# Attention with a depthwise convolution in the queries: low halves ahead of hops, second sums ahead of convolution, fewer taps beside the batches

## The chip, the cores and the metric

The kernel runs on one core of one Trainium2 chip. The metric is device time in microseconds (us) of one execution. A core has TensorE (PE in the rows; PEld is its weight load), VectorE (DVE), ScalarE (ACT), GpSimd (POOL) and SyncE (SP), each with an instruction queue of its own that is worked off in order, and 16 DMA engines that all the issuing queues share. A row marked SPq is SyncE's queue issuing a transfer.

## The reference

All of it is float32: four images of 384 channels and 48 x 48 = 2304 tokens, eight heads of 48 channels.

```python
local = conv(x, conv_w, 7x7, SAME, one filter per channel)       # then scaled and shifted by bn
x_norm = layernorm(x over channels)                              # at each token
q, k, v = split(x_norm @ qkv_w.T + qkv_b)                        # 8 heads of 48
q = q + layernorm(local over channels)
attn = softmax(q @ k.T * 48 ** -0.5)
out = x + (attn @ v) @ proj_w.T + proj_b
```

## The kernel before

**Groups and batches.** Each image's queries are cut into five groups of 8, 10, 10, 10 and 10 rows of 48 tokens (384 or 480 columns). There are 20 groups, t = 0 to 19; image b has groups 5b to 5b + 4. A group works through four pairs of heads with 18 blocks of 128 keys each, in eight batches s = 0 to 7 of nine blocks; pair p has batches 2p and 2p + 1. In a batch TensorE first makes the scores (L1152): keys and queries are split into a high half, which the matmul's short format holds, and the low half that remains, so a block takes six matmuls and nine blocks take 54. ScalarE turns the scores into exponentials (L1168, L1164); in groups from 4 on, DVE copies one half block out of its bank (L1172), and ScalarE works on that copy later. Then TensorE weighs the values with the exponentials (L1189, 36 rows in the profile). Eight banks, taken two at a time, hold the scores.

**Quarters.** The rest of the work is hung into the batches by hand. `steps_of(t)` lists, for batch s and quarter q, what is issued at `(s, q)`: quarter 0 in the middle of the scores, 1 behind the scores, 2 in the middle of the weighing, 3 behind it. TensorE's order is not affected by the quarters' DVE work, but a wait is.

**Key stages.** Between the images ("kv" in the code, t = 5, 10, 15) six groups gk of 384 tokens are projected to values, keys and queries (`from_x`, L730), and the image before gets its output projection and residual (L1126). Each gk has five places h = 0 to 4 for convolution.

**Convolution on DVE.** The 7 x 7 filter is 49 multiply-adds ("taps", L374) per channel chunk, 144 instructions a group after ScalarE's first ones. A planner spreads all 2659 that remain after start-up: `spare` and `spare_at_keys` say how many us of DVE time a quarter or place has beside its other work, in units that are scaled by the group's columns, `due` says by which place a group's taps must be done, and `share` is the number of taps that result.

**The queries' norms.** A query group's convolution is normalized over channels. Groups 1 to 4 take their means by matmul. The groups t + 1 of later images (t = 5 to 8, 10 to 13, 15 to 18) take sums by a *hop*: `sum` (L597, L598), a 32 x 32 transpose and a reduction (L678, L679), then two small transfers on SyncE's queue, `parts<-part` (L682) into DRAM and `four<-parts` (L683) back to all partitions; the second waits on SyncE until the first has landed. DVE then adds the four (L692). There is a first hop for the mean (`q_sum`, read by `few_centre`) and a second for the variance (`sum_squares` and `out`, read by `few_variance`); `few_root` is three small ScalarE instructions (L711 to L713), `few_newton` finishes the root on DVE (L717 to L719), `local_end` (L982) scales, `query_end` (L994) adds the projected query. The norm of the next image's x goes the same way in the key stages and in some groups.

**Query parts.** `high_queries` casts one pair's queries to the short format on ScalarE (L1008); `low_queries` subtracts on DVE (L1013) and issues six transfers (L1018, L1020), on SyncE's queue except for some of the first groups, that put both halves where the matmuls read them (tile qs). Pair p's parts are made during batch 2p - 2, pair 0's at the end of the group before.

**Sums.** The softmax denominators of group t - 1 go through DRAM: den out (L1061), rd in (`sums_in`, L1072), reciprocal and check (L1082, L1086), rden out and rb in (`divide`).

Of the kernel before, what the change touches and what calls it, by code (L numbers as in the profile page):

```python
# [49 lines left out]
def unshifted_pass(  # L50
# [21 lines left out]
    G = RG * W  # L72
# [8 lines left out]
    NA = len(ROWS)  # L81
# [380 lines left out]
    def spare(t, s, q):  # L462
# [4 lines left out]
        time -= {(0, 3): 0.5, (2, 3): 0.5, (4, 3): 0.5}.get((s, q), 0.0)  # L467
        if b + 1 < B and g >= begins(b + 1):
            time -= {
                (1, 3): 2.3, (3, 1): 2.2, (3, 3): 2.3, (5, 0): 0.4, (5, 2): 2.6,  # L470
            }.get((s, q), 0.0)
        if g:
            time -= {(1, 2): 0.6, (5, 1): 1.4}.get((s, q), 0.0)
        if t + 1 < NA:
# [4 lines left out]
            time -= {(6, 3): 3.0, (7, 0): 1.0, (7, 2): 0.5}.get((s, q), 0.0)  # L479
        elif g < NA - 1:  # L480
            time -= {
                (2, 2): 2.3, (4, 0): 2.2, (4, 3): 2.3, (6, 0): 0.4, (6, 2): 2.8, (6, 3): 1.7,
                (7, 0): 0.5,
            }.get((s, q), 0.0)
        return max(0.3, time) * columns_of(t) / G
# [9 lines left out]
    def spare_at_keys(b, g, h):  # L495
        time = 4.6 - {0: 0.6, 2: 0.7, 3: 1.4, 4: 1.2}.get(h, 0.0)
# [30 lines left out]
    share = {}  # L527
# [702 lines left out]
    def steps_of(t):  # L1230
# [13 lines left out]
        for p in range(1, NP):  # L1244
            at(2 * p - 2, 1, lambda p=p: high_queries(t, p))
            at(2 * p - 2, 3, lambda p=p: low_queries(t, p))
        if g:

            def begin():
                ratios[t] = divide(t - 1)  # L1250
# [5 lines left out]

            at(1, 2, begin)
# [34 lines left out]
        if following:  # L1292
# [11 lines left out]
            at(2, 2, q_sum)  # L1304
# [3 lines left out]
            at(6, 0, lambda: norm.few_variance())  # L1308
            at(6, 1, lambda: norm.few_root())
            at(6, 2, q_end)  # L1310
            at(6, 3, lambda: high_queries(t + 1, 0))
            at(7, 0, lambda: low_queries(t + 1, 0))
        if early:
# [26 lines left out]
            at(7, 2, lambda: low_queries(t + 1, 0, other))  # L1340
# [143 lines left out]
    for t in range(NT):  # L1484
        b, g = divmod(t, NA)
        if g == 0 and b:
# [3 lines left out]
            norms_x = {}  # L1490
            for gk in range(NG):
# [25 lines left out]
                if gk == 5:  # L1517
                    norm.few_variance()
                    norm.few_root()
# [3 lines left out]
                convolve("kv", t, gk, 1)  # L1523
# [22 lines left out]
                convolve("kv", t, gk, 4)  # L1546
# [585 lines left out]
```

## Time and profile before

| What | Value |
|---|---|
| Median of 3 runs | 2731.15 us (2725.64 to 2733.86) |
| Profiled execution | 2727.67 us, span 2725.8 us |
| TensorE busy | 2701.5 us, 99% |
| DVE busy | 2345.3 us, 86% |
| ScalarE busy | 1651.8 us, 61% |
| Taps (L374) | 2832, mean 657 ns |

Busy times say how long an engine had an instruction under way. The span is the time from the first to the last instruction. A releaser behind an arrow is what ended a wait; `DMA qs<-qs` is the landing of a transfer that wrote qs. A wait that TensorE does not share costs nothing by itself. TensorE's granted clock is 0.999 over the span.

### The profile page before, as it was taken

The page shows a single profiled execution, that of the slowest core. Times are in us where ns is not written, and L with a number is a line of the kernel's source. Part 1 is how long each engine was busy: PE and PEld are TensorE (multiplying, and loading weights), DVE is VectorE, ACT ScalarE, POOL GpSimd, SP SyncE. Part 2 cuts the span into 40 slices and gives each one's busy share as a digit, 9 for nine tenths or more (in the row PEclk, how much of TensorE's full clock was granted, in tenths as well). Part 3 has the DMA queues.
Part 4 walks back from the last instruction along what each step waited for, and adds up shares of the span by engine and source line. Part 5 has one row for each costly group of instructions (what it writes and reads, how often), then busy time and mean ns, then how long its engine had stood idle before and what let it go on. Part 6 is the DMA issues. An engine that isn't in the chain of part 4 may idle for free.

```text
span 2725.8 us, 45553 instructions
## 1 busy us (share of the span) xinstructions
PE 2701.5 (99%) x16468; PEld 1546.6 (57%) x16468; DVE 2345.3 (86%) x4090; ACT 1651.8 (61%) x2478; POOL 592.1 (22%) x1061
## 2 busy tenths in 40 slices
PE   9999999999999999999999999999999999999999
PEld 6565555555556555555555665555555665555555
DVE  8999999899989999989999999988898899996212
ACT  4366666677325766777632677776752376776662
POOL 3531111112462111010255210101115511101110
PEclk9999999999999999999999999999999999999999
DMA  8454544546456545354555553545635645445442
GB/s 176 91 148 138 136 116 123 135 128 163 109 154 163 140 118 149 109 147 123 149 140 141 167 139 116 140 131 128 157 107 162 164 123 142 135 131 145 133 135 89
DMA packets 160124, 370.42 MB, mean 136 GB/s; under 512 B 58273, under 2 KB 107234, under 8 KB 159890
## 3 DMA queue, kind: packets, MB, share of 16 engines
q0 software_dynamic: 70688, 277.77, 36.2%
q1 hardware_dynamic: 83456, 79.29, 12.8%
q10 hardware_dynamic: 5746, 10.36, 1.2%
q8 instruction: 132, 2.16, 0.4%
q14 instruction: 102, 0.84, 0.1%
HBM read 258.14 MB, written 64.14 MB: 118 GB/s over the span
## 4 chain that ended last, share of the span: by engine, by line
PE 81%; DVE 11%; DMA 5%; SPq 1%; issue 1%; ACT 1%; POOL 0%; DVEq 0%; ACTq 0%; POOLq 0%
PE banks L1189 35%; PE banks L1152 30%; PE banks L730 15%; DVE acc L374 7%; DMA qs<-qs 1%; DMA parts<-part 1%; DMA four<-parts 1%; DMA rd<-den 1%; SPq L1020 0%; DVE pt L841 0%; DVE sq L598 0%; DVE pt L1172 0%; DMA qt<-xn 0%; DVE sq L597 0%; DVE xn L994 0%
## 5 line engine op out<-in xcount | busy, mean ns | idle before, releaser
L374 DVE SCALAR_TENSOR_TENSOR acc<-slab,vec,acc 128x470 f32<-128x470 f32 (+10 forms) x2832 | 1656.5, 657 | 0.4 <-ACT acc L337 0.4
L1189 PE MATMUL banks<-pt,v 128*64 128x480 f32 (+1 forms) x5760 | 1150.1, 553 | 0.0
L1168 ACT ACTIVATE pt<-banks 128x960 f32<-128x960 f32 (+1 forms) x1152 | 1008.2, 946 | 131.1 <-PE banks L1152 78.2
L1152 PE MATMUL banks<-qs,ks 64*128 64x480 f32 (+1 forms) x8640 | 965.2, 374 | 13.1 <-DMA qs<-qs 9.7
L1152 PEld LDWEIGHTS banks<-qs,ks 64*128 64x128 f32 x8640 | 790.3, 184 | 242.1 <-issue 116.5
L1189 PEld LDWEIGHTS banks<-pt,v 128*64 128x64 f32 x5760 | 399.9, 137 | 672.6 <-issue 629.9
L802 POOL DMA_DIRECT2D ks<-wide x220 | 159.8, 726 | 1409.1 <-PE banks L1152 1386.3
L1164 ACT ACTIVATE pt<-banks 128x480 f32<-128x480 f32 (+1 forms) x448 | 256.5, 572 | 141.3 <-PE banks L1189 141.3
L730 PE MATMUL banks<-xn,w_qk 128*128 128x384 f32 x864 | 284.2, 486 | 0.0
L730 PEld LDWEIGHTS banks<-xn,w_qk 128*128 128x128 f32 x864 | 164.0, 190 | 114.7 <-issue 0.7
L1172 DVE COPY pt<-banks 128x480 f32<-128x480 f32 (+1 forms) x128 | 81.6, 638 | 147.3 <-PE banks L1152 145.4
L1037 ACT COPY o<-banks 113x480 f32<-113x480 f32 (+1 forms) x80 | 43.6, 545 | 196.2 <-PE banks L1189 196.1
L730 PE MATMUL banks<-w_v,xn 128*128 128x384 f32 x432 | 145.1, 488 | 3.5 <-DVE xn L725 3.0
L824 ACT COPY v<-banks 128x384 f32<-128x384 f32 x72 | 34.3, 478 | 165.8 <-PE banks L730 165.8
L1047 ACT COPY ao<-banks 113x480 f32<-113x480 f32 (+1 forms) x60 | 32.7, 545 | 141.5 <-PE banks L1189 141.5
L730 PEld LDWEIGHTS banks<-w_v,xn 128*128 128x128 f32 x432 | 81.3, 190 | 62.8 <-DVE xn L725 4.7
L730 PE MATMUL banks<-af,w_o 128*128 128x384 f32 (+1 forms) x270 | 85.2, 470 | 0.0
L1056 DVE TENSOR_TENSOR ao<-ao,o 113x480 f32<-113x480 f32 (+1 forms) x60 | 38.0, 633 | 54.3 <-ACT o L1037 54.3
L787 POOL DMA_DIRECT2D wide<-pt x120 | 59.9, 502 | 108.6 <-ACT pt L838 101.4
L1164 ACT ACTIVATE pt<-pt 128x480 f32<-128x480 f32 (+1 forms) x128 | 80.8, 632 | 0.6 <-DVE pt L1172 0.6
L838 ACT ACTIVATE pt<-banks,qkb 128x384 fp32r<-128x384 f32 x60 | 34.6, 581 | 60.3 <-PE banks L730 55.9
L730 PEld LDWEIGHTS banks<-af,w_o 128*128 128x128 f32 x270 | 51.3, 190 | 31.9
(160 smaller groups left out, 1450.1 us busy)
## 6 DMA issues: line engine op xcount, KB each, us to landing
ks<-wide POOLq DMA_DIRECT2D x220, 768.0 KB, 5.4
qs<-qs SPq DMA_DIRECT2D x346, 60.0 KB
slab<-in_x_dram POOLq DMA_DIRECT2D x22, 432.0 KB, 7.9
wide<-ks POOLq DMA_DIRECT2D x12, 768.0 KB, 5.4
xr<-in_x_dram POOLq DMA_DIRECT2D x16, 576.0 KB, 5.1
rb<-rden SPq DMA_DIRECT2D x32, 270.0 KB
held<-ao POOLq DMA_DIRECT2D x12, 720.0 KB, 4.5
xn<-in_x_dram POOLq DMA_DIRECT2D x36, 216.0 KB, 5.3
```

What stands on the lines that cost most here:

```text
L374: nc.vector.scalar_tensor_tensor(dst, src, weight, dst, ALU.mult, ALU.add)
L730: nc.tensor.matmul(dst, lhsT=weights(c), rhs=src(c), start=c == 0, stop=c == CC - 1)
L787: nc.gpsimd.dma_start(out=last[16 * u : 16 * u + 16, 0], in_=k[r : r + 16, 0])
L802: queue.dma_start(out=place_keys(b, p, i), in_=wide[b, p][:, :, at])
L838: nc.scalar.activation(k[:, 0, :], r[:, :G], AF.Identity, bias=bias)
L1037: nc.scalar.copy(part[0 : 64 + HA], sums[0 : 64 + HA, :n])
L1056: nc.vector.tensor_add(dst, dst, part[0 : 64 + HA])
L1152: nc.tensor.matmul(r[:, j, :n], lhsT=ks[rows, w, at], rhs=qs[rows, m, :], start=n_th == 0, stop=n_th == 2,)
L1164: nc.scalar.activation(weights_of[:, at, :n], src, AF.Exp, scale=SCALE)
L1168: nc.scalar.activation(to, r[:, :, :n], AF.Exp, scale=SCALE)
L1172: nc.vector.tensor_copy(weights_of[:, second, :n], r[:, 1, :n])
L1189: nc.tensor.matmul(sums[halves[j], :n], lhsT=values[t // NA, kb // NB][:, first : first + 64], rhs=weights_of[:, at[j], :n], start=start, ...
```

## The change

1. Low halves of pairs 1 to 3 are issued at quarter 2 of batches 0, 2 and 4 instead of quarter 3, and the query norm's first hop (`q_sum`) at quarter 3 of batch 2 instead of quarter 2.
2. Pair 0 of groups 1 to 4: low halves in the middle of quarter 1's convolution in batch 7 instead of quarter 2. Of the groups with hops: variance at (5, 3) instead of (6, 0), root and end of the query both at (6, 1) instead of (6, 1) and (6, 2), high half at (6, 2) and low half at (6, 3) instead of (6, 3) and (7, 0).
3. `sums_in` is called at (0, 3), `divide` still at (1, 2).
4. Key stages: the second sums and their hop ahead of place 4's convolution, variance and root in the middle of place 1's convolution instead of ahead of it.
5. The planner's costs follow these moves; every quarter from group 5 on has 0.1 less, every place of a key stage 0.2 more.

```diff
         if q == 0:
             time -= 0.5 * (s % 2 == 0) + 0.5 * (t >= NA - 1)
-        time -= {(0, 3): 0.5, (2, 3): 0.5, (4, 3): 0.5}.get((s, q), 0.0)
+        time -= {(0, 2): 0.5, (2, 2): 0.5, (4, 2): 0.5}.get((s, q), 0.0)
...
         elif g < NA - 1:
             time -= {
-                (2, 2): 2.3, (4, 0): 2.2, (4, 3): 2.3, (6, 0): 0.4, (6, 2): 2.8, (6, 3): 1.7,
-                (7, 0): 0.5,
+                (2, 3): 2.5, (4, 0): 2.2, (4, 3): 2.5, (5, 3): 0.4, (6, 1): 2.6, (6, 2): 2.0,
+                (6, 3): 0.5,
             }.get((s, q), 0.0)
-        return max(0.3, time) * columns_of(t) / G
+        time = max(0.3, time) - (0.1 if t >= NA else 0.0)
+        return time * columns_of(t) / G
...
     def spare_at_keys(b, g, h):
-        time = 4.6 - {0: 0.6, 2: 0.7, 3: 1.4, 4: 1.2}.get(h, 0.0)
+        time = 4.8 - {0: 0.6, 2: 0.7, 3: 1.4, 4: 1.2}.get(h, 0.0)
...
-            last = "slot", t - 1, 2, 2
+            last = "slot", t - 1, 2, 3
...
             at(2 * p - 2, 1, lambda p=p: high_queries(t, p))
-            at(2 * p - 2, 3, lambda p=p: low_queries(t, p))
+            at(2 * p - 2, 2, lambda p=p: low_queries(t, p))
         if g:
 
+            def sums():
+                ratios[t] = sums_in(t - 1)
+
             def begin():
-                ratios[t] = divide(t - 1)
+                ratios[t] = divide(t - 1, ratios[t])
...
+            at(0, 3, sums)
             at(1, 2, begin)
...
-            at(2, 2, q_sum)
+            at(2, 3, q_sum)
             at(4, 0, lambda: norm.few_centre())
             at(4, 2, lambda: norm.squares())
             at(4, 3, lambda: norm.sum_squares(), lambda: norm.out())
-            at(6, 0, lambda: norm.few_variance())
-            at(6, 1, lambda: norm.few_root())
-            at(6, 2, q_end)
-            at(6, 3, lambda: high_queries(t + 1, 0))
-            at(7, 0, lambda: low_queries(t + 1, 0))
+            at(5, 3, lambda: norm.few_variance())
+            at(6, 1, lambda: norm.few_root(), q_end)
+            at(6, 2, lambda: high_queries(t + 1, 0))
+            at(6, 3, lambda: low_queries(t + 1, 0))
...
             at(7, 1, lambda: high_queries(t + 1, 0))
-            at(7, 2, lambda: low_queries(t + 1, 0, other))
+            halfway[t, 7, 1] = lambda: low_queries(t + 1, 0, other)
...
                 both(making)
-                if old:
-                    old.few_variance()
-                    old.few_root()
...
-                convolve("kv", t, gk, 1)
+
+                def variance():
+                    for n in (old, norm if gk == 5 else None):
+                        if n:
+                            n.few_variance()
+                            n.few_root()
+
+                convolve("kv", t, gk, 1, at=made + share["kv", t, gk, 1] // 2, then=variance)
...
-                convolve("kv", t, gk, 4)
                 if new is not None:
                     norms_x[gk].sum_squares()
                     norms_x[gk].out()
                 if gk == 4:
                     norm.sum_squares()
                     norm.out()
+                convolve("kv", t, gk, 4)
```

**SyncE's queue, group 13, batches 1 to 3.** The first fence is the kernel before, the second the changed one, whose line numbers are one higher here (L1019 is L1018 before). `qs_2` is the third pair's tile; the 4x32x15 hop is the query norm's, the 4x32x12 one is that of the next image's x.

```order
L1061 DMA den_15502<-ao_15500 1x480 x2
L682 DMA parts<-part 4x32x15
L683 DMA four<-parts 128x1x60
L1018 DMA qs_2_15716<-qs_2_15716 16x960
L1020 DMA qs_2_15716<-qs_2_15716 32x480 x2
L1018 DMA qs_2_15716<-qs_2_15716 16x960
L1020 DMA qs_2_15716<-qs_2_15716 32x480 x2
L682 DMA parts<-part 4x32x12
```

```order
L1062 DMA den_15504<-ao_15502 1x480 x2
L1019 DMA qs_2_15711<-qs_2_15711 16x960
L1021 DMA qs_2_15711<-qs_2_15711 32x480 x2
L1019 DMA qs_2_15711<-qs_2_15711 16x960
L1021 DMA qs_2_15711<-qs_2_15711 32x480 x2
L683 DMA parts<-part 4x32x15
L684 DMA four<-parts 128x1x60
L683 DMA parts<-part 4x32x12
```

The six qs transfers and the norm's first hop have changed places. In all of SyncE's queue this happens twelve times and nothing else moves; `rd<-den` stands where it stood.

**DVE, group 11, batch 6 into batch 7.** The kernel before, then the changed one. L1172 (L1173) is the copy that opens a batch, L717 to L719 the Newton step, `qs_0` the next group's first pair.

```order
L1172 COPY pt<-banks 128x480
L692 TENSOR_REDUCE few<-four 128x15
L706 TENSOR_SCALAR few<-few 128x15
L374 SCALAR_TENSOR_TENSOR acc_13182<-slab_3_12457,vec,acc_13182 128x10x47 x7
L717 TENSOR_TENSOR few_u<-few_u,few 128x15
L718 SCALAR_TENSOR_TENSOR few_y<-few_u,few_y 128x15
L719 STREAM_TRANSPOSE sq<-few_y 128x480
L982 SCALAR_TENSOR_TENSOR acc_11986<-acc_11986,sq 128x1440
L994 SCALAR_TENSOR_TENSOR xn<-acc_11986,vec,xn 128x480 x3
L374 SCALAR_TENSOR_TENSOR acc_13182<-slab_3_12457,vec,acc_13182 128x10x47 x3
L1172 COPY pt<-banks 128x480
L1013 TENSOR_TENSOR qs_0_14276<-xn,qs_0_14276 128x480
```

```order
L1173 COPY pt<-banks 128x480
L374 SCALAR_TENSOR_TENSOR acc_13168<-slab_3_12400,vec,acc_13168 128x10x47 x3
L718 TENSOR_TENSOR few_u<-few_u,few 128x15
L719 SCALAR_TENSOR_TENSOR few_y<-few_u,few_y 128x15
L720 STREAM_TRANSPOSE sq<-few_y 128x480
L983 SCALAR_TENSOR_TENSOR acc_12013<-acc_12013,sq 128x1440
L995 SCALAR_TENSOR_TENSOR xn<-acc_12013,vec,xn 128x480 x3
L374 SCALAR_TENSOR_TENSOR acc_13168<-slab_3_12400,vec,acc_13168 128x10x47 x2
L1014 TENSOR_TENSOR qs_0_14263<-xn,qs_0_14263 128x480
L374 SCALAR_TENSOR_TENSOR acc_13168<-slab_3_12400,vec,acc_13168 128x10x47 x5
L1173 COPY pt<-banks 128x480
```

The variance (L692, L706) has left the batch, the Newton step has three taps ahead of it instead of seven, and the low half has come in ahead of batch 7's copy.

**DVE, image 1's key stage, from gk = 2 into gk = 3.** Before, then changed. `sq<-sq` starts the second sums, L692 with L706 is the variance, `sq<-xn` the next norm's first sum.

```order
L597 TENSOR_TENSOR sq<-sq 128x384
L598 TENSOR_TENSOR sq<-sq 128x384
L678 STREAM_TRANSPOSE sq<-sq 128x384
L679 TENSOR_REDUCE part<-sq 128x12
L1126 SCALAR_TENSOR_TENSOR xr_2_6251<-banks,pb,xr_2_6251 128x384 x2
L374 SCALAR_TENSOR_TENSOR acc_5309<-slab_1_4789,vec,acc_5309 128x10x46 x3
L597 TENSOR_TENSOR sq<-xn 128x384
L598 TENSOR_TENSOR sq<-sq,xn 128x384
L678 STREAM_TRANSPOSE sq<-sq 128x384
L679 TENSOR_REDUCE part<-sq 128x12
L692 TENSOR_REDUCE few<-four 128x12
L706 TENSOR_SCALAR few<-few 128x12
```

```order
L679 STREAM_TRANSPOSE sq<-sq 128x384
L680 TENSOR_REDUCE part<-sq 128x12
L374 SCALAR_TENSOR_TENSOR acc_5240<-slab_1_4723,vec,acc_5240 128x10x45 x2
L1127 SCALAR_TENSOR_TENSOR xr_2_6264<-banks,pb,xr_2_6264 128x384 x2
L374 SCALAR_TENSOR_TENSOR acc_5240<-slab_1_4723,vec,acc_5240 128x10x45 x3
L598 TENSOR_TENSOR sq<-xn 128x384
L599 TENSOR_TENSOR sq<-sq,xn 128x384
L679 STREAM_TRANSPOSE sq<-sq 128x384
L680 TENSOR_REDUCE part<-sq 128x12
L374 SCALAR_TENSOR_TENSOR acc_5240<-slab_1_4723,vec,acc_5240 128x10x45 x3
L693 TENSOR_REDUCE few<-four 128x12
L707 TENSOR_SCALAR few<-few 128x12
```

Two taps of place 4 have moved behind the reduction that starts the hop, and three of place 1 ahead of the variance. The three key stages have 92, 103 and 100 taps before and 103, 117 and 113 in the change.

More of the change, by code (lines that the diff above doesn't have):

```diff
@@ L466, in spare @@
             time -= 0.5 * (s % 2 == 0) + 0.5 * (t >= NA - 1)
-        time -= {(0, 3): 0.5, (2, 3): 0.5, (4, 3): 0.5}.get((s, q), 0.0)
+        time -= {(0, 2): 0.5, (2, 2): 0.5, (4, 2): 0.5}.get((s, q), 0.0)
         if b + 1 < B and g >= begins(b + 1):
             time -= {
-                (1, 3): 2.3, (3, 1): 2.2, (3, 3): 2.3, (5, 0): 0.4, (5, 2): 2.6,
+                (1, 3): 2.5, (3, 1): 2.2, (3, 3): 2.5, (5, 0): 0.4, (5, 2): 2.6,
             }.get((s, q), 0.0)
         if g:
-            time -= {(1, 2): 0.6, (5, 1): 1.4}.get((s, q), 0.0)
+            time -= {(1, 2): 0.8, (5, 1): 1.4}.get((s, q), 0.0)
         if t + 1 < NA:
@@ L1490, in unshifted_pass @@
             norms_x = {}
+            norm = None
             for gk in range(NG):
```

5 lines of the change are left out of this document (1 added, 4 removed).

## The prediction

> **What bounds the kernel now.** First the page's busy times by engine, then two rows of the waits (us in all, times, longest us).
>
> ```profile
> PE 2701.5 (99%) x16468; PEld 1546.6 (57%) x16468; DVE 2345.3 (86%) x4090; ACT 1651.8 (61%) x2478; POOL 592.1 (22%) x1061
> ...
> PE banks L1152 <- DMA qs<-qs: 9.7, 13, 1.6
> ...
> PE banks L1152 <- DVE pt L1172: 2.3, 2, 1.7
> ```
>
> TensorE sets the end: it was idle for 24.3 of 2725.8 us. What it waited for belongs to this change: late query parts (qs) and late copies out of its banks (pt). Since the ends of matmuls are modelled, I size each loss by the distance of starts. The chain of waits in order of time (start, us, what) shows an undisturbed batch and three disturbed places:
>
> ```profile
> 1016.02 7.40 PE banks L1189 x36
> ...
> 1053.20 8.80 DMA rd<-den
> ...
> 1072.17 7.40 PE banks L1189 x36
> ...
> 1166.25 7.40 PE banks L1189 x36
> ...
> 1194.63 8.23 DMA qs<-qs
> 1208.82 7.40 PE banks L1189 x36
> ...
> 1752.79 6.05 PE banks L1152 x54
> 1758.84 7.40 PE banks L1189 x36
> ...
> 1826.07 7.40 PE banks L1189 x36
> 1842.97 8.16 DMA parts<-part
> 1855.01 9.07 DMA qs<-qs
> 1871.38 7.40 PE banks L1189 x36
> ```
>
> A batch takes 6.05 (scores) + 7.40 (weighing) = 13.45. In group 13 the weighing of batches 1 and 4 starts 45.31 apart, three batches (40.35) and 5.0 lost. In group 8 it is 42.57: 2.2 lost. From group 6's batch 6 to group 7's batch 2 it is 56.15 for four batches: 2.4 lost, behind the sums' transfer (rd). Smaller losses stand in TensorE's own order of time:
>
> ```profile
> 360.49 0.48 PE L1152 MATMUL banks<-qs,ks 64*128 64x480 f32 x1
> 361.60 0.70 PE L1152 MATMUL banks<-qs,ks 64*128 64x480 f32 x4 [0.62 <-DMA qs<-qs]
> 362.64 1.56 PE L1152 MATMUL banks<-qs,ks 64*128 64x480 f32 x12 [0.34 <-DMA qs<-qs]
> ...
> 811.68 6.07 PE L730 MATMUL banks<-w_v,xn 128*128 128x384 f32 x18 [2.41 <-DVE xn L725]
> ...
> 880.60 0.79 PE L1152 MATMUL banks<-qs,ks 64*128 64x384 f32 x5
> 882.08 4.66 PE L1152 MATMUL banks<-qs,ks 64*128 64x384 f32 x49 [0.69 <-DMA qs<-qs]
> ...
> 926.55 0.91 PE L1152 MATMUL banks<-qs,ks 64*128 64x480 f32 x5
> 928.09 5.64 PE L1152 MATMUL banks<-qs,ks 64*128 64x480 f32 x49 [0.63 <-DMA qs<-qs]
> ...
> 954.50 4.38 PE L1152 MATMUL banks<-qs,ks 64*128 64x480 f32 x37
> 959.43 2.22 PE L1152 MATMUL banks<-qs,ks 64*128 64x480 f32 x17 [0.55 <-DVE pt L1172]
> 961.59 7.47 PE L1189 MATMUL banks<-pt,v 128*64 128x480 f32 x36
> ```
>
> A score matmul of 480 columns takes 6.05/54 = 0.112. As group 2 opens, five of them from 360.49 should be out by 361.05, but the sixth starts at 362.64: 1.6 lost.
>
> **Part 1, the third pair's low halves ahead of the norm's first hop (groups 5 to 8, 10 to 13, 15 to 18).** Group 13 again, DVE's and the queue's rows:
>
> ```profile
> 1843.38 0.65 DVE L1013 TENSOR_TENSOR qs<-xn,qs 128x480 fp32r<-128x480 f32 x1
> ...
> 1851.81 0.58 SPq L1018 DMA_DIRECT2D qs<-qs  x1
> ...
> 1867.00 0.24 DVE L692 TENSOR_REDUCE few<-four 128x15 f32<-128x60 f32 x1
> ```
>
> The halves were ready at 1844.03, but SyncE stood at the hop's second transfer until its first had landed (8.16 from 1842.97), and issued them from 1851.81. In the changed order they are ahead of the hop: 7.8 earlier, and the subtraction itself comes a quarter earlier. That covers the 5.0, the 2.2, and in group 5 another 1.1 (five matmuls of 384 columns, at 0.112 x 384/480 = 0.09, end 0.45 after 880.60, but the next starts 1.48 after it). Gain 8.3. Bounds: 0, if the transfers' own 8 to 9 us set the end, and 8.3. I take 8.3, since the 7.8 of standing is more than any of the losses.
>
> What is late next is the hop. It starts behind six more issues (0.58 each, 3.5) and, as a quarter is some four taps and the low half, about 3 later. Its reader came 24.0 after the start (1842.97 to 1867.00) and keeps about 17. The longest hop that a DVE wait lets one measure took 9.0 (part 4). Price 0; a hop that took all of the 24 would hold DVE for 7, in groups 8 and 13.
>
> **Part 2, the first pair's low halves.** They move, for groups 1 to 4, from batch 7's third quarter into the middle of its second, and for the groups whose norm uses hops from batch 7 into batch 6's last quarter. In groups 0, 1 and 2 the orders have two, three and four convolution taps fewer ahead of them: at 0.63 a tap (part 4) 1.3, 1.9 and 2.5 earlier. The next groups' openings lost 2.0, 1.6 and 1.4, read as the 1.6 above. Gain 1.3 + 1.6 + 1.4 = 4.3. At group 6 five matmuls from 926.55 end at 927.11 and the sixth starts at 928.09, 1.0 lost; the halves now leave some 3 earlier. Gain 5.3 in all, bounds 2.5 (half the lead arrives) and 5.3.
>
> **Part 3, sums fetched a batch sooner.** In SyncE's order the rd transfer stands behind the same six qs transfers as before, so it issues when it did, at 1053.20. Price 0; bounds -1 and 1, as DVE's order around it shifts by a tap or two (0.63 each).
>
> **Part 4, the second sums ahead of convolution, and the variance in the middle of it (key stages).** Before, DVE came to the hop's result too soon; the last two rows group image 1's key stage by line (count, busy us, mean ns, idle before).
>
> ```profile
> 790.03 0.58 SPq L682 DMA_DIRECT2D parts<-part  x1
> ...
> 799.04 0.23 DVE L692 TENSOR_REDUCE few<-four 128x12 f32<-128x48 f32 x1 [3.92 <-DMA four<-parts]
> ...
> L374 DVE SCALAR_TENSOR_TENSOR acc<-slab,vec,acc 128x470 f32<-128x470 f32 (+3 forms) x109 | 68.6, 694 | 0.0
> L692 DVE TENSOR_REDUCE few<-four 128x12 f32<-128x48 f32 x10 | 2.3, 227 | 12.6 <-DMA four<-parts 12.6
> ```
>
> A tap is 68.6/109 = 0.63. Between hop and reader stood 9.0 - 3.9 = 5.1 of DVE work. Now the two taps that stood before the hop and three or four of the next share stand there too: 5.1 + 6 x 0.63 = 8.9, about the hop. So most of the 12.6 idle us become work, and the xn that TensorE had to wait 2.41 for at 811.68 comes some 3 earlier. Gain 2.4, bounds 0 and 2.4.
>
> [...]
>
> **Part 5, the planner.** The orders move 11, 14 and 13 taps out of the batches into the three later key stages: 6.9, 8.8 and 8.2 us of DVE. Those stages by windows (from:to, us, then busy of PE, PEld, DVE, ACT, POOL):
>
> ```profile
> 686.70:836.50 149.80, 147.39 (x472) 84.40 (x468) 134.21 (x238) 42.83 (x84) 76.45 (x150) 1.00 0.52 134
> 1364.10:1503.50 139.40, 139.40 (x432) 81.90 (x432) 124.52 (x218) 38.94 (x75) 75.88 (x147) 1.00 0.56 145
> 2026.70:2166.20 139.50, 139.50 (x436) 81.98 (x434) 122.09 (x215) 39.19 (x75) 78.97 (x154) 1.00 0.54 144
> ```
>
> DVE was idle there for 15.6, 14.9 and 17.4, so the taps fit and leave 6 to 9; TensorE's projections hide them. Price 0; uncovered it would be 23.9. In the batches groups 5 to 8 shed 5 to 8 taps each, 3 to 5 us. Late copies had cost 1.0 in group 6 (scores from 954.50 to 961.59, 7.09 instead of 6.05) and the 2.4 up to group 7's batch 2. I take 2.0 of this 3.4, as the wait for rd itself remains; bounds 0 and 3.4.
>
> **Part 6, root and Newton step side by side in batch 6.** Group 11's batch 6, and the waits' row for the copies:
>
> ```profile
> 1674.18 0.66 DVE L1172 COPY pt<-banks 128x480 f32<-128x480 f32 x1
> ...
> 1675.12 4.41 DVE L374 SCALAR_TENSOR_TENSOR acc<-slab,vec,acc 128x470 f32<-128x470 f32 x7
> ...
> 1678.29 0.22 ACT L713 ACTIVATE few_u<-few_y 128x15 f32<-128x15 f32 x1
> ...
> DVE pt L1172 <- PE banks L1152: 145.4, 92, 12.9
> ```
>
> ScalarE's root stands behind the batch's first exponentials; it ends at 1678.51, and that does not move. Seven taps filled DVE's time until then; now three lie between the copy and the Newton step, which is reached at 1674.84 + 1.9 = 1676.7. So DVE waits 1.8. Queued behind it are the Newton step, the query's end, the low half (0.65, now in this batch) and the next batch's copy, which frees banks that TensorE needs. The batch grows by 1.8 + 0.65 - 0.4 (the variance has left it) = 2.0. How late may a copy be? In group 6's batch 2 TensorE resumed at 959.43 after a copy of 0.7 us that began 4.2 into the batch, and lost 1.0; the copy above began 2.3 into its batch, whose scores took 6.05. So about 0.9 of lateness is free and up to 1.1 is lost in each of twelve places: bounds 0 and 13. In 92 of the kernel's 128 copies DVE had been waiting for TensorE, so it had reserve; I take a third of the bound, 4.4.
>
> **Sum.** 8.3 + 5.3 + 2.4 + 2.0 = 18.0 gained, 4.4 lost, 13.6 in all. The profiled execution took 2727.67 us (span 2725.8), which makes 2714. The median of the three runs, 2731.15, is 3.5 higher; small qs losses that I left unsized (the 9.7 us are 13 waits) work the other way, so I leave it at 2714.
>
> **Rivals.** A, slower: the key stages have no room. DVE serves banks, norms and residuals there in a fixed order; if every added tap lands between a projection and the instruction that frees its banks, 23.9 show and part 4's 2.4 are lost: 2714 + 26.3 = 2740. For it: TensorE did wait for xn in a stage with DVE at 90%. Against: some 15 idle us in each, and no idle TensorE in the two later ones. It decides once the added taps pass the idle time ahead of the instruction that is needed.
>
> B: the wait for ScalarE costs its full 13 instead of 4.4: 2723. For it: the orders keep as many taps in batches 6 and 7 as before, so the planner gives no relief just there. Against: the 92 copies.
>
> C: transfers stay late. If congestion and not the queue's order makes qs late, part 1 gives nothing: 2722. For it: the chain charges qs itself 8.23 and 9.07. Against: the 7.8 of standing. That the change does less than it says holds for part 3 already.
>
> **How the numbers follow.** Forecast 0.68, B 0.12, C 0.10, A 0.10. A measurement of this kernel tells about 0.3%, 8 us, from no change: faster means below 2723. The bounds of parts 2, 5 and 6 give the forecast 2705 to 2722; reaching over B and C toward A, the range is 2705 to 2729. Faster: nearly all of the forecast and half of B and C, 0.74. Slower: most of A, 0.08. Same: the rest, 0.18.
>
> **What would show it.** Right: no TensorE wait for qs in batch 4 of groups 5, 8 and 13; openings of groups 1 to 3 that lose under 1 us; DVE's idle time at the four transfer in image 1's key stage down from 12.6 to under 4; a DVE wait of some 1.8 for the root in batch 6 of the twelve groups. Wrong: key stages longer than before, copies that cost TensorE over 8 in all, or DVE waiting at the hop's reader in batch 4.

## The result, and the profile after

The changed kernel takes 2714.3 us (median of 4 runs, 2712.2 to 2716.5), the kernel before 2730.3 beside it; the ratio is 0.9939, 95% interval 0.9921 to 0.9956. The forecast was 2714, the range 2705 to 2729. The profiled execution of the changed kernel took 2716.5 us (span 2714.7), the slowest of its four, so between the two profiles the gain is 11.2 us where the medians show 16. Busy times by engine on the changed kernel's page:

```profile
PE 2697.4 (99%) x16468; PEld 1547.1 (57%) x16468; DVE 2345.7 (86%) x4090; ACT 1651.8 (61%) x2478; POOL 591.6 (22%) x1061
```

TensorE's waits in the changed kernel (us in all, times, longest us):

```profile
PE banks L1153 <- DMA qs<-qs: 4.1, 3, 3.2
PE banks L1153 <- DVE pt L1173: 3.0, 4, 1.6
...
PE banks L731 <- DVE xn L726: 0.6, 2, 0.4
```

Waits for query parts fell from 13 (9.7 us) to 3 (4.1), and one of the three is 3.2 long. Waits for late copies did not fall (2.3 to 3.0).

The table is worked out from the distances of TensorE's starts in the two profiles, batch by batch; a stage is counted from the start of the last weighing ahead of it to the first score behind it.

| Place | Before, us | Changed, us | Gain | Forecast term |
|---|---|---|---|---|
| Scores of batch 4, groups 5, 8, 13 | 6.07, 8.28, 11.04 | 5.00, 6.05, 6.06 | 8.3 | part 1: 8.3 |
| Openings of groups 2, 3, 6 | 8.04, 7.80, 7.12 | 6.38, 6.38, 6.02 | 4.2 | part 2: 4.0 |
| Opening of group 1, with the weighing ahead | 14.35 | 18.99 | -4.6 | part 2: 1.3 |
| Image 1's key stage | 149.59 | 146.91 | 2.7 | part 4: 2.4 |
| Scores, group 6 batch 2 and group 7 batch 2 | 7.09, 8.26 | 8.17, 6.05 | 1.1 | part 5: 2.0 |
| Scores, group 5 batch 7, group 10 batch 6, group 15 batch 7 | 5.07, 4.99, 5.06 | 5.73, 5.70, 6.01 | -2.3 | part 6: -4.4 |

The rest, 1.7, is spread over places of 1 us at most.

**Part 1's place.** Group 13 in the changed kernel, SyncE's queue, DVE and TensorE in the timeline:

```profile
1839.59 0.59 SPq L683 DMA_DIRECT2D parts<-part  x1
...
1848.85 0.59 SPq L684 DMA_DIRECT2D four<-parts  x1
...
1853.95 6.13 PE L1153 MATMUL banks<-qs,ks 64*128 64x480 f32 x54
...
1856.81 0.25 DVE L693 TENSOR_REDUCE few<-four 128x15 f32<-128x60 f32 x1
```

SyncE still stands at the hop's second transfer, for 9.3 us now, but the query parts are out ahead of it. Batch 4's scores run through, and the hop's reader comes 17.2 after its start, without a wait.

**Part 6's wait.** Group 11, batch 6, changed kernel, DVE and ScalarE:

```profile
1668.03 0.66 DVE L1173 COPY pt<-banks 128x480 f32<-128x480 f32 x1 [0.83 <-PE banks L1153]
1668.61 1.94 DVE L374 SCALAR_TENSOR_TENSOR acc<-slab,vec,acc 128x470 f32<-128x470 f32 x3
1672.38 0.17 DVE L718 TENSOR_TENSOR few_u<-few_u,few 128x15 f32<-128x15 f32 x1 [1.84 <-ACT few_u L714]
...
1672.14 0.21 ACT L714 ACTIVATE few_u<-few_y 128x15 f32<-128x15 f32 x1
```

DVE waits 1.84, where the prediction worked out 1.8 (in the twelve batches it is 1.0 to 2.6), and TensorE loses nothing in this group.

**Group 1's opening** is the one place that got clearly worse. TensorE's and GpSimd's rows, first the kernel before, then the changed one:

```profile
248.24 7.10 PE L1152 MATMUL banks<-qs,ks 64*128 64x480 f32 x54 [1.29 <-DMA qs<-qs]
...
241.29 0.53 POOL L1020 DMA_DIRECT2D qs<-qs  x1 [2.73 <-ACT qs L1008]
241.82 0.73 POOL L802 DMA_DIRECT2D ks<-wide  x1
246.08 0.52 POOL L1018 DMA_DIRECT2D qs<-qs  x1 [3.53 <-DVE qs L1013]
```

```profile
247.68 0.97 PE L1153 MATMUL banks<-qs,ks 64*128 64x480 f32 x4
251.87 8.76 PE L1153 MATMUL banks<-qs,ks 64*128 64x480 f32 x50 [3.23 <-DMA qs<-qs]
...
241.94 0.52 POOL L1021 DMA_DIRECT2D qs<-qs  x1 [2.73 <-ACT qs L1009]
245.51 0.51 POOL L1019 DMA_DIRECT2D qs<-qs  x1 [3.05 <-DVE qs L1014]
246.06 0.76 POOL L803 DMA_DIRECT2D ks<-wide  x1
246.81 0.51 POOL L1021 DMA_DIRECT2D qs<-qs  x1
```

In this group half of the query parts go over GpSimd's queue. Before, the keys' load (`ks<-wide`, 768 KB) was issued at 241.82 and the qs transfer that waits for DVE stood behind it. Now that qs transfer stands ahead of the load and holds it for 3.05 us, so the load starts 4.2 later, right in front of the last qs transfer. Some 3.2 of the loss is clock: the granted clock is 0.50 from 251.4 to 258.2 here, with TensorE at work for 6.3 of these 6.8 us, and it was 1.00 in the kernel before.

### The profile page after: what moved, and what is told of

It is laid out like the page before. It is cut to its first block, busy times and chain, and to the rows that moved or that the text cites. A ratio compares the mean times of both kernels' runs of the same rounds, so it can differ in the third digit from the quotient of the medians.

```text
span 2714.7 us, 45559 instructions
## 1 busy us (share of the span) xinstructions
PE 2697.4 (99%) x16468; PEld 1547.1 (57%) x16468; DVE 2345.7 (86%) x4090; ACT 1651.8 (61%) x2478; POOL 591.6 (22%) x1061
## 3 DMA queue, kind: packets, MB, share of 16 engines
q1 hardware_dynamic: 83456, 79.29, 12.9%
## 4 chain that ended last, share of the span: by engine, by line
PE 93%; DVE 3%; DMA 2%; SPq 1%; ACT 0%; issue 0%; POOL 0%; DVEq 0%; ACTq 0%
PE banks L1190 40%; PE banks L1153 33%; PE banks L731 19%; DVE acc L374 2%; DMA xn<-in_x_dram 1%; DMA staged<-in_qkv_wT_dram 0%; SPq L395 0%; PE banks L621 0%; DMA qs<-qs 0%; DMA rd<-den 0%; DVE xn L995 0%; ACT pt L1169 0%; DMA parts<-part 0%; DVE acc L983 0%; DVE pt L842 0%
## 5 line engine op out<-in xcount | busy, mean ns | idle before, releaser
L1173 DVE COPY pt<-banks 128x480 f32<-128x480 f32 (+1 forms) x128 | 81.6, 638 | 134.4 <-PE banks L1153 131.7
```

The source lines that it names most:

```text
L1173: nc.vector.tensor_copy(weights_of[:, second, :n], r[:, 1, :n])
```

## The experiments

The theory: the prediction's six parts, each at its price, with group 1's loss caused by GpSimd's queue. The rival for each part: the gain is not its own, but comes from other parts or from chance in when transfers land. Differences are taken to the 2713.3 us of the changed kernel as it ran again with the first of them. The kernel before had 2729.1, 2730.6 and 2729.1 in the three comparisons, so a difference across these is uncertain by 1 to 2 us. Some waits of TensorE come with 3.4 or 6.8 us at a granted clock of 0.50 (last section) and then cost up to as much again (group 1's opening: 3.23 of wait, some 3.2 of clock); the text says where that bears on a difference.

### The changed kernel unchanged

> The changed kernel unaltered, to see which of its waits come back in another execution. Theory 'queue order': the opening of group 1 loses about 6.5 us again (TensorE waits some 3 us for qs, then runs at a lower granted clock), because the keys' transfer now stands between two of the first pair's transfers in GpSimd's queue; total 2712 to 2717. Rival 'chance': the opening of group 1 loses about 1 us this time and the wait was one execution's; total near 2709 to 2712.

Measured: 2713.3 us (2712.9 to 2714.0), ratio to before 0.994 (0.9924 to 0.9957). Group 1's opening lost 3.2 beside the kernel before in this profile, with the clock at 0.50 for 3.4 us instead of 6.8, and group 6's batch 2 took 6.20 instead of 8.17. So the first is there each time (3.0 to 3.4 in the five other profiles that leave this place as it is), and the second is mostly chance.

### Part 1 undone

```diff
-            at(2 * p - 2, 2, lambda p=p: low_queries(t, p))
+            at(2 * p - 2, 3, lambda p=p: low_queries(t, p))
...
-            at(2, 3, q_sum)
+            at(2, 2, q_sum)
```

> The changed kernel with part 1 undone: low halves of pairs 1 to 3 at quarter 3 and the query norm's first hop at quarter 2 again, planner as changed. Theory 'queue order': waits for qs in batch 4 come back in some groups, 5 to 11 us in all, total 2720 to 2726. Rival 'late transfers': qs lands when congestion lets it, the total stays within 3 us of the changed kernel, 2712 to 2717.

Measured: 2717.6 us (2715.4 to 2720.0), ratio 0.9955 (0.9939 to 0.9972): 4.3 above the changed kernel. Batch 4 of groups 5, 8 and 13 stayed undisturbed (5.00, 6.09, 6.05), although the hop was ahead of the query parts again. What cost most in the profiled execution was group 2's batch 4 (10.30), where no hop stands in the queue and TensorE waited for keys, by its row in this kernel (the clock fell here too, to 0.50 for 3.4 us):

```profile
426.26 3.78 PE L1153 MATMUL banks<-qs,ks 64*128 64x480 f32 x18 [2.42 <-DMA ks<-wide]
```

Why the hop did no harm here is in SyncE's and GpSimd's rows of group 13, this kernel first, then the kernel before:

```profile
1838.83 0.56 SPq L683 DMA_DIRECT2D parts<-part  x1
1840.86 0.56 SPq L684 DMA_DIRECT2D four<-parts  x1
...
1840.93 1.69 POOL L123 DMA_DIRECT2D slab<-in_x_dram  x3 [7.14 <-DVE acc L374]
```

```profile
1840.59 2.20 POOL L123 DMA_DIRECT2D slab<-in_x_dram  x4 [1.97 <-DVE acc L374]
...
1842.97 0.56 SPq L682 DMA_DIRECT2D parts<-part  x1
1851.15 0.56 SPq L683 DMA_DIRECT2D four<-parts  x1
```

The slab loads (two of 432 KB, two of 144 KB) bring the rows that convolution reads, and they are issued when DVE has done the last tap on the old slab. In the kernel before they started 2.4 us ahead of the hop's first transfer, which then took 8.2 us. Here they started 2.1 behind it, and it took 2.0. The reason is that this run does not undo part 1 alone. Its planner still counts with the hop at quarter 3 (`last` is `(2, 3)`), so it leaves taps of the next group to quarter 2, where the sums now stand ahead of them. DVE's rows show it, this kernel first, then the changed one:

```profile
1836.05 0.66 DVE L598 TENSOR_TENSOR sq<-acc 128x480 f32<-128x480 f32 x1
...
1838.72 1.91 DVE L374 SCALAR_TENSOR_TENSOR acc<-slab,vec,acc 128x315 f32<-128x315 f32 x4
```

```profile
1834.99 1.91 DVE L374 SCALAR_TENSOR_TENSOR acc<-slab,vec,acc 128x315 f32<-128x315 f32 x4
1836.82 0.65 DVE L598 TENSOR_TENSOR sq<-acc 128x480 f32<-128x480 f32 x1
```

These four taps are the last of group 14's convolution. In the changed kernel the sums follow them; here they come behind the sums, so this kernel leaves four taps out of the sums that it takes in groups 13 and 18 and five out of those in group 8. The slab loads, which wait for the last tap, therefore start behind the hop. So the 4.3 is not the price of part 1, and the next run is its test. What the run does show: where the slab loads start behind the hop, in group 13, the old order of the queue costs batch 4 nothing.

### Part 1 alone

The kernel before with the two lines of part 1 and the planner's costs for these two moves.

> The kernel before with part 1 alone: low halves of pairs 1 to 3 a quarter earlier, the query norm's first hop a quarter later, and the planner told of these two moves only. By the prediction's term it gains 8.3, which is about 2722 beside 2730 for the kernel before; batch 4 of groups 5, 8 and 13 then loses under 0.5 us in TensorE's order of time. By the price that undoing the part has shown (4.3) it gains about 4, 2726. The rival is that the late transfers are mostly chance, which the undone run hints at, since groups 8 and 13 were undisturbed there: then the gain is under 2, 2728 to 2731.

Measured (third comparison): 2717.2 us (2715.9 to 2718.2), ratio 0.9962 (0.9949 to 0.9975): 12.0 less than the kernel before (2729.1). In the profiles batch 4 of groups 5, 8 and 13 gains 8.1 (5.00, 6.25 and 6.05 now), which is the prediction's 8.3. The sums stand behind the last tap here, so in group 13 four slab loads were issued 2.4 to 0.7 us ahead of the hop's first transfer, and it took 8.7 (from 1838.48); batch 4 runs through all the same, since its query parts are out. It also gains 2.6 in image 1's key stage (147.04) and 3.0 in batch 2 of groups 6 and 7 (6.05, 6.34), and loses 2.7 in the openings of groups 4, 11, 16 and in the last group. The rival of chance falls. Part 1's term holds where it was put, and the part brings more at places that it was not priced for; the planner's lines for the two moves come with it and were not run by themselves.

The part also takes away scatter: 22 runs of the kernel before lie between 2721.5 and 2734.1, five of this one within 2.2 us. The scatter goes with the granted clock. Of the 22, the three at 1.000 took 2722.2 to 2725.9 and the three at 0.997 took 2731.6 to 2734.1; the mean is 0.9985, and 0.9996 here. By that some 3 of the 12.0 are clock, an estimate ((0.9996 - 0.9985) x 2729).

### Part 4 undone

```diff
+                if old:
+                    old.few_variance()
+                    old.few_root()
...
-                convolve("kv", t, gk, 1, at=made + share["kv", t, gk, 1] // 2, then=variance)
+                convolve("kv", t, gk, 1)
...
+                convolve("kv", t, gk, 4)
                 if new is not None:
                     norms_x[gk].sum_squares()
                     norms_x[gk].out()
...
-                convolve("kv", t, gk, 4)
```

> The changed kernel with part 4 undone: in the key stages the second sums behind place 4's convolution and the variance ahead of place 1's, planner as changed (11 to 14 taps more in each stage than before). Theory 'the hop's wait was made work': DVE idles 10 us or more at the four transfer in image 1's key stage again, and with the added taps the wait for xn grows beyond 2.4; total 3 to 8 us above the changed kernel, 2717 to 2722. Rival 'key stages had room anyway': no more than 1 us above, 2714 to 2716.

Measured: 2722.1 us (2720.0 to 2725.1), ratio 0.997 (0.9958 to 0.9983): 8.8 above the changed kernel. In the profiled execution, the slowest of its six, image 1's stage takes 6.8 longer, with the clock at 0.50 for 6.8 us (from 813.2), and batch 2 of group 16 takes 3.6 longer, with the clock at 0.50 for 3.4.

### Part 4 alone

The kernel before with part 4's edits and nothing else.

> The kernel before with part 4 alone: in the key stages the second sums ahead of place 4's convolution and the variance in the middle of place 1's, the planner as before. By the prediction's term it gains 2.4, 2728, all of it in image 1's stage, whose wait for xn (2.41 us) is gone. By the price of undoing it in the changed kernel (8.8) it is about 2721; I expect the former, since the 8.8 was measured with 11 to 14 more taps in each stage, which pushed the reader of the hop and the projections' banks later. Waits of DVE for the second transfer of the hops in image 1's stage fall from 12.6 us in all to under 6.

Measured (third comparison): 2724.1 us (2721.8 to 2727.2), ratio 0.9986 (0.9976 to 0.9997): 5.0 less than before, of which image 1's stage has 2.7 (146.91). DVE's idle time at the hop's reader in this stage falls from 12.6 to 5.3. Most of the rest of the difference between the profiles is group 13's batch 4, 7.97 instead of 11.04 and without a fall of the clock; part 4 moves nothing there, so this is probably chance.

### The planner's two levels undone

```diff
-        time = max(0.3, time) - (0.1 if t >= NA else 0.0)
+        time = max(0.3, time)
...
-        time = 4.8 - {0: 0.6, 2: 0.7, 3: 1.4, 4: 1.2}.get(h, 0.0)
+        time = 4.6 - {0: 0.6, 2: 0.7, 3: 1.4, 4: 1.2}.get(h, 0.0)
```

> The changed kernel with the planner's two general amounts undone (0.1 less in a quarter from group 5 on, 0.2 more in a place of a key stage); its other costs as changed. Theory 'relief where DVE was full': copies come late again in groups 5 to 8 and TensorE loses 3 to 8 us there, total 2717 to 2722. Rival 'the other parts did it': within 2 us of the changed kernel.

Measured (second comparison): 2724.6 us (2721.4 to 2729.8), ratio 0.9981 (0.9971 to 0.999): 11.3 above the changed kernel. Batch 2 of groups 6 and 7 took 10.65 and 10.11, where the changed kernel's two profiles have 8.17 and 6.20 in the one and 6.05 in the other. Four pieces of its chain of waits, and TensorE's rows at the two places:

```profile
944.15 5.30 DMA rd<-den
...
1015.40 0.23 ACT few_u L714
...
1025.93 12.92 DVE acc L374 x21
...
1052.85 9.73 DMA rd<-den
```

```profile
957.60 3.72 PE L1153 MATMUL banks<-qs,ks 64*128 64x480 f32 x17 [2.61 <-DVE pt L1173]
...
1069.84 2.58 PE L1153 MATMUL banks<-qs,ks 64*128 64x480 f32 x14 [2.42 <-DVE pt L1173]
```

This is the chain that the prediction had as "late copies", grown: DVE is late as the group opens, so the sums go out late, `rd` comes back late, DVE waits for it, and the copy that TensorE needs stands behind. In group 6 the chain leads from ScalarE's root (1015.40) by way of 21 taps to group 7's late sums and their transfer at 1052.85. So with more taps in the batches the waits of part 6 do cost TensorE time; how much of the 11.3 goes through the root is not shown. Some of it is clock again: at both places it fell to 0.50 for 3.4 us, so the 17 and 14 scores took 3.72 and 2.58, where 1.9 and 1.6 are usual.

### The planner's levels alone

The kernel before with only those two lines of the planner.

> The kernel before with the planner's two general levels alone (0.1 less in each quarter from group 5 on, 0.2 more in each place of a key stage), and no instruction moved beside the convolution. Two prices stand: the prediction's 2.0 and the 11.3 that undoing the levels cost in the changed kernel. If the levels are worth something by themselves, because batches lose late copies and the key stages have room, the time is about 2719. If their price in the changed kernel is that of its own moves, which fill batches 6 and 2 and need the relief, this kernel gains 0 to 3, 2727 to 2730, and image 1's key stage, without part 4, gets longer than 149.6 us by the taps added, up to 5.

Measured (third comparison): 2733.2 us (2730.7 to 2737.0), ratio 1.0019 (1.0009 to 1.0028): 4.1 slower than before. Image 1's stage grew to 153.41. Two views of that stage, DVE's groups by line and TensorE's waits:

```profile
L374 DVE SCALAR_TENSOR_TENSOR acc<-slab,vec,acc 128x470 f32<-128x470 f32 (+3 forms) x120 | 75.3, 694 | 0.0
L693 DVE TENSOR_REDUCE few<-four 128x12 f32<-128x48 f32 x10 | 2.3, 229 | 8.4 <-DMA four<-parts 8.4
...
PE banks L731 <- DVE xn L726: 4.0, 3, 2.9
```

Beside that, group 11's opening took 13.46 instead of 6.04, by TensorE's and GpSimd's rows:

```profile
1591.85 0.73 PE L1153 MATMUL banks<-qs,ks 64*128 64x480 f32 x4 [1.18 <-DMA qs<-qs]
1596.54 7.17 PE L1153 MATMUL banks<-qs,ks 64*128 64x480 f32 x49 [3.96 <-DMA qs<-qs]
...
1583.18 1.11 POOL L123 DMA_DIRECT2D slab<-in_x_dram  x2 [1.10 <-DVE acc L374]
...
1585.34 1.10 POOL L123 DMA_DIRECT2D slab<-in_x_dram  x2
```

The last qs transfer was issued at 1585.5 among four slab loads and landed 11.0 later. Group 6's batch 2 and 5 and group 7's batch 2, on the other hand, were undisturbed (6.05 each). Part 1's collision stayed: batch 4 of groups 8 and 13 took 9.97 and 8.52, and the hop's first transfer 7.5 and 7.8, behind the slab loads. The clock fell in image 1's stage (3.4 us from 814.7), in group 8 (3.4) and in group 11's opening (6.8).

**Parts 4 and 5 together.** Image 1's stage in the profiles, us:

| | Planner's levels as before | Planner's levels changed |
|---|---|---|
| Order as before | 149.59 | 153.41 (alone), 153.69 (part 4 undone) |
| Part 4's order | 146.91 (alone), 146.91 (levels undone) | 146.91 |

The added taps are free behind part 4's order and cost 4 without it, some 2 of it as waits and the rest as clock: with the levels alone TensorE worked through 3.4 us at 0.50, which loses 1.7, and with part 4 undone it worked for 4.9 of 6.8 us at 0.50, which loses up to 2.5. DVE's groups in this stage, changed kernel:

```profile
L374 DVE SCALAR_TENSOR_TENSOR acc<-slab,vec,acc 128x460 f32<-128x460 f32 (+3 forms) x117 | 73.9, 694 | 0.0
L693 DVE TENSOR_REDUCE few<-four 128x12 f32<-128x48 f32 x10 | 2.3, 226 | 1.4 <-DMA four<-parts 1.4
```

With the levels alone DVE idled for 8.4 us at the reader of the hop, here for 1.4. The 8.4 are time that the taps could not use, since the reader stands ahead of them in DVE's queue, and the xn that TensorE waits for comes behind all of it.

### Group 1's low halves back in quarter 2

```diff
-            halfway[t, 7, 1] = lambda: low_queries(t + 1, 0, other)
+            if t:
+                halfway[t, 7, 1] = lambda: low_queries(t + 1, 0, other)
+            else:
+                at(7, 2, lambda: low_queries(t + 1, 0, other))
```

> The changed kernel with the first pair's low halves of group 1 alone back in batch 7's quarter 2, which puts the keys' transfer ahead of them in GpSimd's queue again. Theory 'queue order': the opening of group 1 loses 2.0 us as before the change instead of 6.5, total 4 to 5 us below the changed kernel, 2709 to 2710. Rival 'chance': no difference to the changed kernel beyond 1.5 us.

Measured: 2711.7 us (2710.6 to 2712.8), ratio 0.9935 (0.9918 to 0.9952): 1.6 less than the changed kernel. Group 1 opens in 14.37 with the weighing ahead of it, as in the kernel before. So part 2 is a loss at group 1, shown by undoing it there alone. 4 to 5 were expected, from the first profile, in which the clock fell for twice as long as in the others; in the second the opening had lost 3.2, and the time gains half of that. Where the rest goes is open.

### Group 1's first query parts all on SyncE's queue

```diff
-            other = nc.sync if 0 < t < NA - 2 else nc.gpsimd
+            other = nc.sync if t < NA - 2 else nc.gpsimd
```

> The changed kernel with all six of group 1's first qs transfers on SyncE's queue, none on GpSimd's. Theory 'queue order': six issues take SyncE 3.6 us from 245.2, so the last starts at about 248.3 and the opening of group 1 loses 1 to 3 us, and the keys' transfer may still share the DMA engines; total 3 to 5 us below the changed kernel, 2709 to 2711. Rival 'the lead alone': the opening loses over 5 us whatever the queue, as the keys' transfer is in the air at the same time.

Measured (second comparison): 2711.6 us (2711.3 to 2712.0), ratio 0.9934 (0.9917 to 0.995). The opening takes 14.82, 4.2 less than in the changed kernel's first profile and 2.7 less than in its second: with nothing ahead of it in GpSimd's queue the keys' load is early again (242.20). It does not become free: TensorE still waits 1.38 and 0.38 for qs, whose last halves now leave one behind the other.

### Both, and the halves earlier still

Group 1's low halves directly behind their cast (by the prediction's own rule, taps ahead of them cost 0.63 each), and all on SyncE's queue.

```diff
-            other = nc.sync if 0 < t < NA - 2 else nc.gpsimd
+            other = nc.sync if t < NA - 2 else nc.gpsimd
...
-            halfway[t, 7, 1] = lambda: low_queries(t + 1, 0, other)
+            if t:
+                halfway[t, 7, 1] = lambda: low_queries(t + 1, 0, other)
+            else:
+                at(7, 1, lambda: low_queries(t + 1, 0, other))
```

> The changed kernel with group 1's first low halves at the start of the quarter, directly behind their cast, and all six transfers on SyncE's queue, so that GpSimd's queue holds none that can stand ahead of the keys' load. If that queue is why group 1 opens 5.1 to 6.5 us late, the opening loses under 1 us here (scores from first to last under 7.1 us) and the time is 2708 to 2710, where the changed kernel has 2713 to 2714. If the transfers land late for another reason, the load of 768 KB beside them above all, the opening loses 2 to 3 us as with SyncE's queue alone, and the time is 2711 to 2712.

Measured (third comparison): 2709.9 us (2708.7 to 2710.9), ratio 0.9934 (0.992 to 0.9947). TensorE's and GpSimd's rows of the opening:

```profile
249.18 6.86 PE L1153 MATMUL banks<-qs,ks 64*128 64x480 f32 x54 [1.05 <-DMA qs<-qs]
...
242.47 0.72 POOL L803 DMA_DIRECT2D ks<-wide  x1 [2.73 <-PE banks L1153]
```

The load is issued at 242.47 instead of 246.06, and the opening takes 13.87, 1.5 above an undisturbed one (a weighing of 384 columns, 5.96, and scores of 6.38), where under 1 was expected; why is open. This is the fastest kernel of the study. Its runs lie 3.4 under those of the changed kernel again, but the ratios' intervals overlap, so the step beyond the changed kernel is likely and not proved.

### The root ahead of the exponentials

```diff
-            at(6, 1, lambda: norm.few_root(), q_end)
+            at(6, 0, lambda: norm.few_root())
+            at(6, 1, q_end)
```

> The changed kernel with the norm's root issued at quarter 0 of batch 6, so that on ScalarE it stands ahead of the batch's fifth exponential. It measures part 6. Theory 'reserve': DVE's waits of 1.0 to 2.6 us for the root in twelve batches fall under 0.5, and the total falls by only 1 to 3 us, as copies came late enough to cost TensorE only in the 384-column groups 5, 10 and 15; 2711 to 2714. Rival 'full price': it falls by 6 us or more. A third way: the root holds exponentials up behind it and TensorE waits for banks, total above the changed kernel.

Measured (second comparison): 2718.1 us (2717.0 to 2719.2), ratio 0.9958 (0.9942 to 0.9975): 4.8 above the changed kernel. In batch 6 of group 11 ScalarE's and TensorE's rows read:

```profile
1667.62 0.23 ACT L712 ACTIVATE few_u<-few 128x15 f32<-128x15 f32 x1
...
1668.14 0.21 ACT L714 ACTIVATE few_u<-few_y 128x15 f32<-128x15 f32 x1
...
1669.27 0.92 PE L1153 MATMUL banks<-qs,ks 64*128 64x480 f32 x6 [0.25 <-ACT pt L1169]
```

DVE no longer waits for the root there, but three small instructions between the exponentials make these later, and batch 6 takes 6.55 to 6.56 instead of 6.05 in all nine groups of 480 columns: 4.5 in all. DVE's wait was the cheaper place for the same work.

### Sums fetched ahead of the second pair's parts

```diff
-            at(0, 3, sums)
+            at(0, 1, sums)
```

> The changed kernel with the sums' fetch at quarter 1 of batch 0, ahead of the second pair's six qs transfers in SyncE's queue, which the change did not do. Theory 'behind six issues': the rd transfer issues some 3.7 us sooner, DVE's waits for it (0.5 to 2.8 us in groups 3 to 17) vanish or fall under 0.5, the 2.1 us that group 6's batch 2 loses goes; total 2 to 3 us below the changed kernel, 2711 to 2712. Rival 'the sums come late themselves': the waits stay and the total does not move by 1 us.

Measured (second comparison): 2714.0 us (2712.3 to 2714.9), ratio 0.9943 (0.9926 to 0.9959). DVE's waits for rd, in this kernel and, behind it, in the changed one:

```profile
DVE rd L1083 <- DMA rd<-den: 0.8, 1, 0.8
```

```profile
DVE rd L1083 <- DMA rd<-den: 10.8, 9, 2.8
```

Here the call does move the transfer in SyncE's queue; the waits go, and the time stays. They were waits of an engine with reserve.

## Why the prediction was right, and where it was not

**Part 1: right.** Mechanism and size stand: 8.3 in the two profiles, 8.1 with the part alone. The prediction named the order of SyncE's queue as the cause and did not ask why the hop's first transfer took 8.16 at all; the slab loads issued just ahead of it were the other half of the cause, as group 13 shows (8.2 with them ahead, 2.0 with them behind). Rival C, under which part 1 would bring nothing, is out.

**Part 2: right for groups 2, 3 and 6 (4.2 against 4.0), wrong for group 1**, where the step "1.3 earlier, so 1.3 gained" failed: a loss of 4.6 in the profile, 3.2 in the second one. By these places the part as a whole is worth between -0.4 and 1.0, not 5.3. The prediction counted the taps ahead of the subtraction on DVE and left out the other queue that the transfers pass, GpSimd's, where the earlier subtraction put a waiting transfer ahead of the keys' load.

**Part 3: right.** The `rd` transfer did not move in SyncE's queue, and the experiment that does move the transfer gains nothing.

**Part 4: right on the stage (2.7 against 2.4, DVE's idle time 12.6 to 1.4), undersized on its worth.** With the added taps in place, undoing it costs 8.8, of which image 1's stage has 6.8 (153.69 against 146.91) in the profile, up to 2.5 of it clock. The prediction priced it against the old taps.

**Part 5: undersized, 2.0 against 11.3 when undone.** "The key stages hide the taps" holds only behind part 4's order; without it rival A's mechanism is real, at 4 rather than 24 us. And "2.0 of the late copies' 3.4" took the kernel before as the yardstick, while the batches to be relieved are those of the changed kernel, in which part 6 makes DVE later. The chain through the root speaks for that; no run separates it. The prediction also left out the granted clock, which with the levels undone stood at 0.50 for 3.4 us at each of the two waits for copies (2.61 and 2.42).

**Part 6: the wait was right (1.8 worked out, 1.84 seen), its price half of the forecast (2.3 against 4.4) and put elsewhere.** The nine groups of 480 columns lost nothing, so DVE's reserve covers a batch that is 2.0 longer. The three groups of 384 columns lost 0.7 to 1.0 each. With the root ahead of the exponentials group 15's batch 7 fell from 6.01 to 4.97, while its batch 6 rose from 5.00 to 5.58; group 5's batch 7 stayed at 5.69, so there the cause is open. Rival B is out.

That the sum came out within 1 us is partly luck, because the errors cancelled: group 1 came out 5.9 short of its term and parts 3, 4 and 5 within 1 us of theirs in the profiles, while part 6 cost 2.1 less and the medians gained 4.8 more than the two profiles. The bounds of parts 2, 5 and 6 add up to 2708 to 2727, not to the 2705 to 2722 that the prediction writes; the result lies in both. Of the signs that it named for being right, one failed: group 1's opening.

**The parts are not independent.** Alone, parts 1 and 4 and the planner's levels bring 12.0, 5.0 and -4.1, 12.9 together; the whole change gains 16. Undone one at a time, part 4 and the levels cost 8.8 and 11.3, more than they bring alone: the levels need part 4, so each is worth more with the other. What part 1 costs when it alone is undone stays open. Parts 2 and 6 were not undone as a whole, and what they bring over all groups stays open too.

## What to carry to other kernels

When an instruction moves, list what stands behind it on every queue that it issues to, not only on the engine that computes: an earlier subtraction put a small waiting transfer ahead of a large load and cost 4.6 us. When a small transfer takes four times as long as its like (8.2 against 2.0 us in group 13), look for the large loads issued just ahead of it and for what releases them. When one line of a planned order is undone, undo what the planner was told of it too, or the run measures something else, here sums that leave out four taps. And price slack that one edit frees and another fills as a pair, in both orders; a part measured alone can even have the wrong sign.

## What the hardware showed beyond that

**The granted clock stood at 0.50 for 6.8 us from late in a wait of 3.23, and for 3.4 us behind two waits of 1.60 and 1.06 close together.** Group 1's opening in the changed kernel, by windows (from:to, us, busy of PE, PEld, DVE, ACT, POOL, then clock, DMA share, GB/s), and group 13's in the kernel before:

```profile
252.00:256.00 4.00, 4.00 (x20) 3.76 (x22) 4.00 (x8) 2.49 (x3) 0.00 (x0) 0.50 0.08 20
256.00:262.00 6.00, 6.00 (x41) 4.73 (x39) 4.80 (x9) 3.69 (x6) 0.75 (x1) 0.82 0.36 88
```

```profile
1860.00:1865.00 5.00, 2.34 (x15) 1.27 (x15) 2.41 (x5) 0.86 (x2) 0.00 (x0) 1.00 0.41 90
1865.00:1870.00 5.00, 5.00 (x36) 4.33 (x34) 3.50 (x5) 4.15 (x6) 0.27 (x1) 0.66 0.03 6
```

In the changed kernel the clock is at 0.50 from 251.4, 2.7 us into TensorE's wait of 3.23, to 258.2, so the 50 scores behind it took 8.76 us where 50 x 0.112 = 5.6 is usual: some 3.2 beside the wait, which doubled the loss. In group 13 the two waits were followed by 0.50 from 1865.2 to 1868.6 (0.66 is the mean of the 5 us), and 49 scores took 7.26 instead of 5.5. So of the 5.0 that part 1 won there, some 1.8 were clock. Behind a wait of 2.42 the clock stood at 0.50 too (part 1 undone, from 426.35), and behind the one of 2.41 for xn that the prediction shows it stayed at 1.00.

**In groups 8 and 13 the hop's first transfer, of 7.5 KB, took 7.5 to 9.6 us with slab loads issued just ahead of it and 2.0 to 2.1 without.** In group 13 it took, from its issue to the second's, 2.0 (slab loads behind it, the run with part 1 undone), 8.2 (ahead of it, kernel before) and 9.3 (ahead of it, changed kernel). In groups 8 and 13 of all fourteen profiles it took 7.5 to 9.6 wherever slab loads were issued in the 2.4 us ahead of it, and 2.0 to 2.1 in the one kernel without.
